# A graph-quantile layer whose engine order is planned: new durations, an order of readers of a PSUM tile, two more pairs scaled on VectorE, and the first sign tiles on ScalarE

## The chip, the cores and the metric

The kernel runs on one core of a Trainium2 chip. The metric is the device time of one execution in microseconds (us); lower is better. The core has these engines: PE (TensorE, matmuls, with its weight load shown as PEld), DVE (VectorE), ACT (ScalarE), POOL (GpSimd), and SP (SyncE, which here only issues transfers). Every engine works through its own list of instructions in order, and waits on semaphores where an instruction needs what another engine makes.

## The reference: what is computed

The input is x (16 graphs, 1024 nodes, 64 values) and a symmetric adjacency with some 8 neighbours and the node itself per row. Cut to what matters:

```python
h = jnp.maximum(_layernorm(x, axis=-1), 0.0)
# drop edges of rows with many neighbours
rem = neigh & (sk > 1) & (rank % sk == sk - 1) & mask[:, :, None]
rem = rem | jnp.swapaxes(rem, 1, 2)
nd = where(rem, 0, adj) > 0
# per node and value: quantiles over the neighbours that are left
s = jnp.sort(where(nd[..., None], h[:, None], inf), axis=2)
for tau, w in zip((0.25, 0.5, 0.75), (0.25, 0.5, 0.25)):
    pos = tau * (nv - 1)
    agg += w * interpolate(s, pos)
# a small MLP and the residual
y = relu((h + agg) @ W1 + b1) @ W2 + b2
out = x + y * mask
```

## The kernel before

The 16 graphs are worked on one after another as batches, and two batches form a pair m (0 to 7). For each batch, `prepare` (L1733) strings these together:

- `load` (L898): eight adjacency tiles of 128 rows arrive by DMA (tile `at`, or `spare` for early ones). Each is turned into signs `sg`, by ACT (L910) or, for every other tile of batch 0 (`fast and t % 2`), by POOL (L908). PE transposes the signs into a PSUM tile `tp` (L917, L923), and ACT (L930), or DVE (L928) for half of the first batch, writes it as `ne`.
- `number` and `drop`: PE counts (`cp`, `nb`) and ranks the neighbours (`rk`, L987 and L992), ACT takes a distance `dist` (L997), DVE decides which edges go (`rem`, L998).
- `keep`: PE combines this with its transpose (`kp`, L1015), ACT writes `kept` (L1020), PE counts again (`code`, L1023), ACT packs the result (`pack`, L1028). `order` makes a permutation `perm` (DVE, L1069) that puts nodes with many neighbours first.
- `collect` (L1073): for each of eight groups k of 128 nodes, nine matmuls (L1090, L1094) fill a PSUM tile `codeP`, of which there are two buffers. ACT copies three parts of it out (`st` L1099, `own` L1103 and L1104), and DVE finds the largest keys (MAX8 L1109, MATCH_REPLACE L1111). From the keys DVE makes `found`, `cand` and at last `idx` (L1138), the list of neighbours.

`fetch` and `issue` then gather the neighbours' rows into tiles `g` (POOL's indirect DMAs, L1281, 952 of them). The groups k are cut into classes (0), (1,2,3), (4,5), (6,7) with ever fewer slots for neighbours; the first two classes are half 0 of the pair, the last two half 1. `aggregate` (L1445) does half 1 first and then half 0. In it `sort` (L1366) runs a network of compare and exchange over the slots on DVE (L1386, L1389, L1394), multiplies the sorted slots by coefficients, and lets PE add them up in a PSUM tile `acc` (L1415). The multiplication has two forms: one DVE TENSOR_TENSOR for several slots (L1411), or, with `by_act`, one ACT ACTIVATE for each 64 columns (L1409). `by_act` is `m >= ACTP`, and `ACTP` is 3, so pairs 0 to 2 multiply on DVE and pairs 3 to 7 on ACT. `opened` adds a one-column MEMSET of `pause` (L805) behind each such DVE operation. As soon as half 1 of a pair has been done, its tiles are gathered anew for the next pair. `aggregate_group` does the same once for eight graphs' longest lists (tile `gg`), and `mlp` (L1551) and `output` (L1602) end a batch.

`weave` interleaves, in the program, the aggregation of pair m−1 with the preparation of pair m+1. This program order isn't what the engines run. `arrange` (L644) reads every instruction emitted, makes a `Step` of each (L605) with a duration `busy` and a delay `lag` to its readers (`cost`, L617), and works out what each must wait for: `before` (must have finished) and `behind` (must have been placed). Then it walks through time once. At each moment, on each engine, the step that is ready and comes first in program order goes next. A ready list may be left for `PATIENCE` ns in favour of a much earlier step, and `PATIENCE` is 0.0. The sequence found is then fixed on every engine by order-only dependencies. So the durations written in `cost`, and the dependencies, decide in which order each engine runs. Two reads of a tile have no order among them in `before`.

Of the kernel before, what the change touches and what calls it, by code (L numbers as in the profile page):

```python
# [33 lines left out]
BF16 = mybir.dt.bfloat16  # L34
# [11 lines left out]
C = 64  # L46
# [24 lines left out]
GROUP = 8  # L71
SLICE = P // GROUP
SECOND = 14
PATIENCE, AHEAD = 0.0, 200


TURNED = (0, 1, 3, 2, 0, 1, 3, 2)
# [472 lines left out]


LOADB, KEEPB, NORMB = 0, 3, 3
ACTP, ACTB = 3, 13
ENGINES = ("PE", "ACT", "DVE", "POOL", "SP")
NAMES = {"PE": "PE", "DVE": "DVE", "Activation": "ACT", "Pool": "POOL", "SP": "SP"}

# [48 lines left out]
class Step:  # L605

    def __init__(self, ins, place):
        self.ins, self.place, self.kind = ins, place, type(ins).__name__
        self.engine = NAMES[str(ins.engine).split(".")[-1]]
        self.reads, self.writes = (  # L610
            [Use(a.bass_ap) for a in aps if getattr(a, "bass_ap", None) is not None] for aps in (ins.ins, ins.outs)
        )
        self.moves = self.kind == "InstDMACopy"
        self.before, self.behind, self.after, self.tail = set(), set(), [], []
        self.busy, self.lag = self.cost()

    def cost(self):  # L617
        sides = self.writes + self.reads
        most = max([u.count for u in sides] or [1])
        if self.engine == "PE":  # L620
            n, lines = self.writes[0].count, self.writes[0].lines
            if any(u.size == 4 for u in self.reads):
                busy = 60 + n if n < 512 else 850
            else:
                busy = max(25, n / 2.4 + 3)
            return busy * 1.15 / (4 if lines[1] - lines[0] <= 32 else 2 if lines[1] - lines[0] <= 64 else 1), 200
        if self.engine == "ACT":
            columns = sum(u.count == 1 and u.size == 4 for u in self.reads) if most > 1 else 0
            return 55 + 0.87 * most + 75 * columns + (170 if len(self.writes) > 1 else 0), 150
        if self.engine == "DVE":  # L630
            psum = any(u.psum for u in sides)
            wide = [u for u in self.reads if u.count > 1]
            if self.kind == "InstTensorTensor" and all(u.size == 2 for u in sides):
                most /= 2
            elif self.kind in ("InstTensorScalarPtr", "InstTensorCopy") and not psum and len(wide) < 2:
                most = most / (4 if max(u.size for u in wide + self.writes) == 2 else 2) + 60
            return (most + 66) / 0.96 + (60 if psum else 0), 80
        if self.engine == "POOL":
            return (1330, 950) if self.moves else (300 if most <= 128 else 1000, 100)
        by = self.writes[0].size * self.writes[0].count * (self.writes[0].lines[1] - self.writes[0].lines[0])  # L640
        return 480, 1500 + by / 300


def arrange(tc, runs, loose, tails, paced):  # L644
# [15 lines left out]
    for s in steps:  # L660
        for u in s.reads + s.writes:
            name = u.tile.name
            for o, other in written.get(name, ()):
                if u.meets(other):
                    s.before.add(o.place)
            if u in s.writes:
                for o, other in read.get(name, ()):
                    if u.meets(other):
                        s.before.add(o.place)
        for u in s.writes:  # L670
            for table in (written, read):
                table[u.tile.name] = [e for e in table.get(u.tile.name, ()) if not u.covers(e[1])]
            written[u.tile.name].append((s, u))
        for u in s.reads:
            read.setdefault(u.tile.name, []).append((s, u))
        for u in s.reads + s.writes:
            if getattr(u.tile, "tag", None):
                if u.tile.name not in users:
                    order.setdefault(u.tile.tag, []).append(u.tile)
                users.setdefault(u.tile.name, []).append(s)  # L680
# [16 lines left out]
    for s in steps:  # L697
        s.behind -= s.before
        s.before.discard(s.place)
        s.behind.discard(s.place)  # L700
        s.left, s.ready = len(s.before) + len(s.behind), 0.0
        for p in (*s.before, *s.behind):
            steps[p].after.append(s)

    free, wire = dict.fromkeys(ENGINES, 0.0), 0.0
    waiting, able, sequence = ({e: [] for e in ENGINES} for _ in range(3))
    for s in steps:
        if not s.left:
            heappush(waiting[s.engine], (0.0, s.place))
    done = 0  # L710
    while done < len(steps):
        when, e = min(
            (free[e] if able[e] else max(free[e], waiting[e][0][0]), e) for e in ENGINES if able[e] or waiting[e]
        )
        while waiting[e] and waiting[e][0][0] <= when:
            heappush(able[e], heappop(waiting[e])[1])
        s = steps[heappop(able[e])]
        if waiting[e] and waiting[e][0][0] < when + PATIENCE and waiting[e][0][1] < s.place - AHEAD:
            heappush(able[e], s.place)
            free[e] = waiting[e][0][0]  # L720
            continue
        done += 1
        sequence[e].append(s)
        free[e] = when + s.busy
        if e == "SP":
            wire = max(wire, free[e]) + s.lag - 1500
            s.lag = wire + 1500 - free[e]
        for o in s.after:
            if s.place in o.behind:
                least = when  # L730
            else:
                least = free[e] + (s.lag + 60 if o.engine != e or s.moves else 115 if e == "DVE" else 0)
            o.ready = max(o.ready, least)
            o.left -= 1
            if not o.left:
                heappush(waiting[o.engine], (o.ready, o.place))
        for q in ENGINES:
            while waiting[q] and waiting[q][0][0] <= free[q]:
                heappush(able[q], heappop(waiting[q])[1])

    for k, s in enumerate(s for s in sequence["POOL"] if s.ins.name in paced[1]):
        if k > 1:
# [16 lines left out]
def list_layer(  # L759
# [138 lines left out]
    def load(b, fast=False):  # L898
# [4 lines left out]
        for t in range(NT):  # L903
            ask(b, t)
            at = asked.pop((b, t))
            sg = wk.tile([P, N], BF16, name="sg")
            if fast and t % 2:
                nc.gpsimd.tensor_scalar(sg, at, 0.0, None, OP.is_gt)  # L908
            else:
                nc.scalar.activation(sg, at, AF.Sign)  # L910
            ask(*divmod(b * NT + t + 2, NT))
            for n in range(2):
                tp = psum.tile([P, 4, P], F32, name="tp", tag="mx", bufs=3)
                run = []
                for s in range(4):
                    m = 4 * n + s
                    run.append(nc.tensor.matmul(  # L917
                        tp[:, s], sg[:, m * P:(m + 1) * P], ident16, start=(s == 0), stop=(s == 3 and t // 4 != n),
                        skip_group_check=True,
                    ))  # L920
                if t // 4 == n:
                    run.append(
                        nc.tensor.matmul(tp[:, t % 4], minus16, ident16, start=False, stop=True, skip_group_check=True)  # L923
                    )
                settle(run)
                to = ne[:, 4 * n:4 * n + 4, t * P:(t + 1) * P]
                if b <= LOADB and n:
                    nc.vector.tensor_scalar(to, tp, 0.0, None, OP.max, saturate=False)  # L928
                else:
                    nc.scalar.activation(to, tp, AF.Relu, saturate=False)  # L930
            if fast and t == 3:
                number(b, 0, 4)
            yield 0.1
# [139 lines left out]
    def collect(b, parts=((0, NT),)):  # L1073
# [12 lines left out]
        for first, last in parts:  # L1086
            for k in range(first, last):
# [5 lines left out]
                for t in range(NT):  # L1093
# [2 lines left out]
                        skip_group_check=True,  # L1096
                    ))
                settle(run)
                nc.scalar.copy(st[:, k], flat[:, OWN:VALUES])  # L1099
                halves, bytes_ = (  # L1100
                    own[:, k, b % 2].bitcast(d).rearrange("p (c k) -> p c k", c=C) for d in (BF16, U8)
                )
                nc.scalar.copy(halves[:, :, 1], flat[:, VALUES:VALUES + C])  # L1103
                nc.scalar.copy(bytes_[:, :, 0:2], flat[:, VALUES + C:].rearrange("p (c k) -> p c k", k=2))  # L1104
                left = code[:, :, :16]
                rest = wk.tile([P, NT, 16], F32, name="rest", bufs=1)
                lo, hi = PASSED[k], PASSED[k + 1]
                for at in range(lo, hi, 8):
                    nc.vector.max(keys[:, at:at + 8], left)  # L1109
                    if at + 8 < hi:  # L1110
                        nc.vector.match_replace(rest, keys[:, at:at + 8], left, 0.0)  # L1111
                        left = rest
                yield 0.4 * (hi - lo) / 4 - 0.4

            part = slice(PASSED[first], PASSED[last])
# [880 lines left out]
```

## Time and profile before

| | |
|---|---|
| Time, median of 9 runs | 2614.96 us (2608.6 to 2624.9) |
| The profiled execution: its time | 2607.81 us |
| The profiled execution: its span | 2605.9 us |
| Instructions | 30392 |
| Mean granted TensorE clock | 0.709 |
| DMA | 121.68 MB, 47 GB/s on average |
| ACT multiplications (L1409) | 560, 148.0 us, mean 350 ns |
| DVE multiplications of `g` (L1411) | 69, of 256 or 384 columns |
| DVE exchanges (L1389, L1394) | 659 each, 309.7 and 308.3 us |
| Sign tiles: on ACT, on POOL | 124, 1063 ns median; 4, 2766 to 2785 ns |

The span is what the profiler saw from the first to the last instruction; the time is of the same execution, with what lies around it. In a profile a row of a group reads: line, engine, operation, out<-in with shapes, x count | busy us, mean ns of one | idle us of the engine just before, and what ended most of it. "remote" in such a place is a semaphore update that comes from nothing the profile shows. The chain of waits follows the work that ended last back through time.

### The profile page before, as it was taken

The numbers are of one execution on the slowest core, as the hardware profiler recorded it, in microseconds if no ns is written. First come the engines' busy times: TensorE is split into PE (matmuls) and PEld (weight loads), VectorE is DVE, ScalarE is ACT, GpSimd is POOL, SyncE is SP. The second block draws the span as 40 slices with busy tenths as digits, with TensorE's granted clock in tenths as the row PEclk, the third lists the DMA queues.
The fourth block names the chain that finished last, engine by engine and source line by source line (L and its number), as shares of the span: only waits on it lengthen the run. The fifth ranks groups of instructions, "written<-read, shape, count | busy, mean of one in ns | idle before, by whom it ended". The sixth has DMA issues, their size and how long they took to land.

```text
span 2605.9 us, 30392 instructions
## 1 busy us (share of the span) xinstructions
PE 1226.3 (47%) x9011; PEld 762.2 (29%) x9011; DVE 1204.5 (46%) x5777; ACT 1109.5 (43%) x3089; POOL 966.3 (37%) x995
## 2 busy tenths in 40 slices
PE   7154346154806283163825436165392352653456
PEld 4133123032404141142413213153151121342334
DVE  5123167143507372193507704078373170529496
ACT  6154255144606262253606625056382242513375
POOL 1714432553262417415370244602507424430400
PEclk9577678586958586585958658576695675876778
DMA  5222122121212121122212112121121001100000
GB/s 171 63 76 68 39 72 60 37 57 49 59 29 86 19 64 40 41 74 52 60 27 80 44 18 60 25 67 37 46 61 42 16 14 22 31 16 1 17 17 11
DMA packets 128833, 121.68 MB, mean 47 GB/s; under 512 B 95730, under 2 KB 96274, under 8 KB 128658
## 3 DMA queue, kind: packets, MB, share of 16 engines
q1 hardware_dynamic: 97106, 87.29, 11.2%
q0 software_dynamic: 31552, 32.36, 6.3%
q8 instruction: 73, 1.20, 0.2%
q14 instruction: 102, 0.84, 0.1%
HBM read 108.79 MB, written 9.05 MB: 45 GB/s over the span
## 4 chain that ended last, share of the span: by engine, by line
another core or an unknown queue 28%; ACT 17%; PE 17%; issue 16%; DVE 6%; DMA 0%; DVEq 0%; SPq 0%; ACTq 0%
ACT dist L997 3%; PE codeP L1094 3%; ACT g L1409 2%; PE acc L1415 2%; ACT kept L1020 2%; ACT sg L910 2%; DVE g L1394 2%; ACT ne L930 1%; DVE g L1389 1%; PE rk L992 1%; PE tp L917 1%; PE rk L987 1%; PE kp L1015 1%; PE high L1537 1%
## 5 line engine op out<-in xcount | busy, mean ns | idle before, releaser
L1281 POOL DMA_INDIRECT g<-gtab,idx x952 | 920.6, 967 | 1393.7 <-issue 725.2
L1389 DVE TENSOR_TENSOR g<-g 128x256 f32<-128x256 f32 (+3 forms) x659 | 309.7, 491 | 63.6 <-PE tp L917 30.7
L1394 DVE TENSOR_TENSOR g<-g 128x256 f32<-128x256 f32 (+3 forms) x659 | 308.3, 490 | 22.4 <-remote 8.5
L997 ACT ACTIVATE dist<-rk,bias 128x512 f16<-128x512 f32 x256 | 169.9, 698 | 271.9 <-remote 198.0
L930 ACT ACTIVATE ne<-tp 128x512 fp8e4<-128x512 f32 x248 | 141.1, 607 | 318.2 <-remote 245.4
L917 PE MATMUL tp<-kb,sg 128*128 128x128 bf16 x1024 | 118.0, 257 | 292.1 <-ACT dist L997 143.3
L987 PE MATMUL rk<-kb,cnt 128*128 128x512 bf16 x256 | 120.0, 469 | 276.7 <-ACT dist L997 138.3
L998 DVE TENSOR_SCALAR rem<-dist,half 128x1024 bf16<-128x1024 f16 x128 | 62.6, 490 | 377.5 <-ACT dist L997 368.9
L1094 PE MATMUL codeP<-pack,perm 128*128 128x332 bf16 x1024 | 198.7, 339 | 11.8 <-DVE perm L1069 11.7
L1020 ACT ACTIVATE kept<-kp 128x512 fp8e4<-128x512 f32 x224 | 135.0, 616 | 144.8 <-remote 88.4
L992 PEld LDWEIGHTS <-ne 128*128 128x128 fp8e4 x1024 | 96.3, 115 | 341.4 <-issue 322.6
L917 PEld LDWEIGHTS <-sg 128*128 128x128 bf16 x1024 | 89.1, 118 | 318.5 <-issue 188.1
L1409 ACT ACTIVATE g<-g,coef 128x64 f32<-128x64 f32 x560 | 148.0, 350 | 56.7 <-DVE g L1389 38.2
L1415 PE MATMUL acc<-g,kf 128*128 128x128 f32 (+2 forms) x472 | 137.9, 425 | 54.2 <-ACT g L1409 37.3
L1023 PE MATMUL code<-kw,kept 128*128 128x17 fp8e5 x1024 | 65.2, 173 | 137.8 <-ACT kept L1020 74.7
L910 ACT ACTIVATE sg<-at 128x1024 bf16<-128x1024 f32 x121 | 126.6, 1075 | 3.6 <-DMA at<-in_adj_dram 3.5
L992 PE MATMUL rk<-kw,ne 128*128 128x128 fp8e5 x1024 | 126.1, 254 | 0.0
L1109 DVE MAX8 keys<-codeP 128x8 f32<-128x128 f32 x128 | 37.9, 296 | 189.0 <-ACT own L1104 92.8
L1094 PEld LDWEIGHTS <-perm 128*128 128x128 bf16 x1024 | 99.3, 107 | 81.5 <-DVE perm L1069 30.4
L805 DVE MEMSET pause<- 128x1 bf16 x1997 | 117.8, 59 | 3.0 <-issue 3.0
L1099 ACT CAST st<-codeP 128x4 bf16<-128x4 f32 x128 | 21.4, 167 | 225.6 <-remote 111.4
L1023 PEld LDWEIGHTS <-kept 128*128 128x128 fp8e4 x1024 | 52.1, 97 | 195.5 <-ACT kept L1020 112.6
(204 smaller groups left out, 2612.4 us busy)
## 6 DMA issues: line engine op xcount, KB each, us to landing
at<-in_adj_dram SPq DMA_DIRECT2D x122, 512.0 KB
g<-gtab,idx POOLq DMA_INDIRECT x952
xt<-in_x_dram SPq DMA_DIRECT2D x16, 256.0 KB
y<-in_x_dram SPq DMA_DIRECT2D x16, 256.0 KB
gtab<-xt SPq DMA_DIRECT2D x16, 256.0 KB
out_dram<-y SPq DMA_DIRECT2D x14, 256.0 KB
spare<-in_adj_dram SPq DMA_DIRECT2D x6, 512.0 KB
gg<-g SPq DMA_DIRECT2D x32, 48.0 KB
```

The costliest lines, as they stand in the source:

```text
L910: nc.scalar.activation(sg, at, AF.Sign)
L917: run.append(nc.tensor.matmul(tp[:, s], sg[:, m * P:(m + 1) * P], ident16, start=(s == 0), stop=(s == 3 and t // 4 != n), skip_group_check ...
L930: nc.scalar.activation(to, tp, AF.Relu, saturate=False)
L992: run.append(nc.tensor.matmul(rk[:, s * P:(s + 1) * P], ne[:, 4 * n + s, ts], upper, start=False, stop=(s == 3), skip_group_check=True,))
L997: nc.scalar.activation(dist[:, n * HALF:(n + 1) * HALF], rk, AF.Abs, bias=bias[:, t:t + 1])
L1020: nc.scalar.activation(kept[:, 4 * n:4 * n + 4], kp, AF.Relu, saturate=False)
L1094: run.append(nc.tensor.matmul(flat, perm[:, t, k * P:(k + 1) * P], pack[:, t], start=False, stop=(t == NT - 1), skip_group_check=True,))
L1281: ins = nc.gpsimd.indirect_dma_start(out=gathered[m, tiles][:, slot, k - lo, h], out_offset=None, in_=tables[2 * m + h][0], in_offset=bass ...
L1389: nc.vector.tensor_tensor(at(f + k * df, df, many), pa, pb, OP.min if what == "<" else OP.max)
L1394: nc.vector.tensor_tensor(pa if back else pb, pa, pb, OP.max if what == "<" else OP.min)
L1409: nc.scalar.activation(v[:, i, j], v[:, i, j], AF.Copy, scale=w[:, i, j:j + 1])
L1415: nc.tensor.matmul(acc, ident32, lines[:, s], start=False, stop=(s == now[-1] and not ends), skip_group_check=True)
```

## The change

It has four parts.

1. `ACTP` becomes 5: pairs 3 and 4 also multiply on DVE.
2. The four sign tiles of batch 0 that POOL made are made by ACT.
3. In `collect`, DVE's MAX8 and MATCH_REPLACE on a `codeP` tile are emitted ahead of ACT's three copies.
4. In `arrange`, reads of one PSUM tile are put in program order: an earlier read by another engine must have finished, one by the same engine must have been placed. With part 3, ACT's copies of a `codeP` tile so come after DVE's reads of it. The durations in `cost` are changed for float32 matmuls, ACT, and POOL. The walk is written anew as `spread`, used by `forward` and `backward`; with `ROUNDS` at 1 it runs forward once with ranks equal to program order, and what `backward` returns isn't used. `PATIENCE` and `AHEAD` go.

```diff
-PATIENCE, AHEAD = 0.0, 200
+ROUNDS = 1
...
-ACTP, ACTB = 3, 13
+ACTP, ACTB = 5, 13
...
         self.busy, self.lag = self.cost()
+        self.load = self.lag - 1500
...
-                busy = 60 + n if n < 512 else 850
+                busy = 4 * max(56, n / 2.4)
...
-            return 55 + 0.87 * most + 75 * columns + (170 if len(self.writes) > 1 else 0), 150
+            inside = 0 if any(u.psum for u in self.reads) else 45
+            return 50 + 0.83 * most + 93 * columns + inside + (170 if len(self.writes) > 1 else 0), 150
...
-            return (1330, 950) if self.moves else (300 if most <= 128 else 1000, 100)
+            return (1345, 950) if self.moves else (300 if most <= 128 else 4100, 100)
...
+def spread(steps, waits, ranks, place):
+
+    free = dict.fromkeys(ENGINES, 0.0)
+    waiting, able = ({e: [] for e in ENGINES} for _ in range(2))
+
+    def free_to_go(p, ready):
+        heappush(waiting[steps[p].engine], (ready, ranks[p], p))
+
+    for s in steps:
+        if not waits[s.place]:
+            free_to_go(s.place, 0.0)
+    for _ in steps:
+        when, e = min(
+            (free[e] if able[e] else max(free[e], waiting[e][0][0]), e) for e in ENGINES if able[e] or waiting[e]
+        )
+        while waiting[e] and waiting[e][0][0] <= when:
+            heappush(able[e], heappop(waiting[e])[1:])
+        s = steps[heappop(able[e])[1]]
+        free[e] = when + s.busy
+        place(s, when, free_to_go)
+    return max(free.values())
...
-            if u in s.writes:
-                for o, other in read.get(name, ()):
-                    if u.meets(other):
-                        s.before.add(o.place)
+            for o, other in read.get(name, ()) if u in s.writes or u.psum else ():
+                if u.meets(other):
+                    (s.before if u in s.writes or o.engine != s.engine else s.behind).add(o.place)
...
-    free, wire = dict.fromkeys(ENGINES, 0.0), 0.0
...
+    ranks, best = [float(s.place) for s in steps], None
+    for _ in range(ROUNDS):
+        sequence, starts, total = forward(steps, ranks)
+        if best is None or total < best[0]:
+            best = total, sequence
+        ranks = backward(steps, starts)
+    sequence = best[1]
...
-            if fast and t % 2:
-                nc.gpsimd.tensor_scalar(sg, at, 0.0, None, OP.is_gt)
-            else:
-                nc.scalar.activation(sg, at, AF.Sign)
+            nc.scalar.activation(sg, at, AF.Sign)
...
-                nc.scalar.copy(st[:, k], flat[:, OWN:VALUES])
-                halves, bytes_ = (
-                    own[:, k, b % 2].bitcast(d).rearrange("p (c k) -> p c k", c=C) for d in (BF16, U8)
-                )
-                nc.scalar.copy(halves[:, :, 1], flat[:, VALUES:VALUES + C])
-                nc.scalar.copy(bytes_[:, :, 0:2], flat[:, VALUES + C:].rearrange("p (c k) -> p c k", k=2))
                 left = code[:, :, :16]
...
                         left = rest
+                nc.scalar.copy(st[:, k], flat[:, OWN:VALUES])
+                halves, bytes_ = (
+                    own[:, k, b % 2].bitcast(d).rearrange("p (c k) -> p c k", c=C) for d in (BF16, U8)
+                )
+                nc.scalar.copy(halves[:, :, 1], flat[:, VALUES:VALUES + C])
+                nc.scalar.copy(bytes_[:, :, 0:2], flat[:, VALUES + C:].rearrange("p (c k) -> p c k", k=2))
```

More of the change, by code (lines that the diff above doesn't have):

```diff
@@ new lines, in between, with forward, place @@
+def between(s, o):
+    return s.lag + 60 if o.engine != s.engine or s.moves else 115 if s.engine == "DVE" else 0
+def forward(steps, ranks):
+    left, ready = [len(s.before) + len(s.behind) for s in steps], [0.0] * len(steps)
+    starts, sequence, wire = [0.0] * len(steps), {e: [] for e in ENGINES}, [0.0]
+    def place(s, when, free_to_go):
+        starts[s.place] = when
+        sequence[s.engine].append(s)
+        end = when + s.busy
+        if s.engine == "SP":
+            wire[0] = max(wire[0], end) + s.load
+            s.lag = wire[0] + 1500 - end
+        for o in s.after:
+            ready[o.place] = max(ready[o.place], when if s.place in o.behind else end + between(s, o))
+            left[o.place] -= 1
+            if not left[o.place]:
+                free_to_go(o.place, ready[o.place])
+    total = spread(steps, list(left), ranks, place)
+    return sequence, starts, total
@@ new lines, in backward, with place @@
+def backward(steps, starts):
+    left, ready, ends = [len(s.after) for s in steps], [0.0] * len(steps), [0.0] * len(steps)
+    def place(s, when, free_to_go):
+        ends[s.place] = when + s.busy
+        for p in (*s.before, *s.behind):
+            o = steps[p]
+            ready[p] = max(ready[p], when + s.busy - o.busy if p in s.behind else when + s.busy + between(o, s))
+            left[p] -= 1
+            if not left[p]:
+                free_to_go(p, ready[p])
+    spread(steps, list(left), [-(starts[s.place] + s.busy) for s in steps], place)
+    return [-t for t in ends]
@@ L700, in arrange @@
         s.behind.discard(s.place)
-        s.left, s.ready = len(s.before) + len(s.behind), 0.0
         for p in (*s.before, *s.behind):
             steps[p].after.append(s)
-    free, wire = dict.fromkeys(ENGINES, 0.0), 0.0
[L706 to L713, printed above, removed]
-        )
[L715 to L730, printed above, removed]
-            else:
[L732 to L739, printed above, removed]
+    ranks, best = [float(s.place) for s in steps], None
[5 more added lines that the diff above has]
+    sequence = best[1]
     for k, s in enumerate(s for s in sequence["POOL"] if s.ins.name in paced[1]):
@@ L906, in load @@
             sg = wk.tile([P, N], BF16, name="sg")
-            if fast and t % 2:
-                nc.gpsimd.tensor_scalar(sg, at, 0.0, None, OP.is_gt)
-            else:
-                nc.scalar.activation(sg, at, AF.Sign)
+            nc.scalar.activation(sg, at, AF.Sign)
             ask(*divmod(b * NT + t + 2, NT))
@@ L1098, in collect @@
                 settle(run)
-                nc.scalar.copy(st[:, k], flat[:, OWN:VALUES])
-                halves, bytes_ = (
-                    own[:, k, b % 2].bitcast(d).rearrange("p (c k) -> p c k", c=C) for d in (BF16, U8)
-                )
-                nc.scalar.copy(halves[:, :, 1], flat[:, VALUES:VALUES + C])
-                nc.scalar.copy(bytes_[:, :, 0:2], flat[:, VALUES + C:].rearrange("p (c k) -> p c k", k=2))
                 left = code[:, :, :16]
```

## The prediction

> **What bounds it.** I read the page's busy shares first, then the groups, then cut the span at the ends of the gathers and asked for the busy time of each stretch.
>
> ```profile
> PE 1226.3 (47%) x9011; PEld 762.2 (29%) x9011; DVE 1204.5 (46%) x5777; ACT 1109.5 (43%) x3089; POOL 966.3 (37%) x995
> ...
> another core or an unknown queue 28%; ACT 17%; PE 17%; issue 16%; DVE 6%; DMA 0%; DVEq 0%; SPq 0%; ACTq 0%
> ...
> L1281 POOL DMA_INDIRECT g<-gtab,idx x952 | 920.6, 967 | 1393.7 <-issue 725.2
> ...
> L1409 ACT ACTIVATE g<-g,coef 128x64 f32<-128x64 f32 x560 | 148.0, 350 | 56.7 <-DVE g L1389 38.2
> ...
> L1109 DVE MAX8 keys<-codeP 128x8 f32<-128x128 f32 x128 | 37.9, 296 | 189.0 <-ACT own L1104 92.8
> ```
>
> No engine is half busy, and over a quarter of the chain belongs to no visible queue. The 952 gathers come in 22 bursts, one gather per 1.25 to 1.33 us, about 1264 us in all. In a burst the rest nearly stands still, as waits such as this show:
>
> ```profile
> 752.26 0.43 DVE L1611 TENSOR_TENSOR yp<-yp,mask 128x256 f32<-128x256 f32 x1 [41.31 <-remote]
> ```
>
> The matmul it reads ended at about 711, and DVE moved only after the burst of 693 to 777 was well under way. Sorting, which waits for no matmul, does run in bursts. So the time is 1264 us of gathers, which the change leaves alone, and about 1342 us between them. That part is to be read. Columns: stretch, length, then busy us (count) of PE, PEld, DVE, ACT, POOL, then clock, DMA share, GB/s.
>
> ```profile
> 1084.20:1158.70 74.50, 45.31 (x415) 31.34 (x414) 59.71 (x310) 42.94 (x91) 0.00 (x0) 0.80 0.26 77
> 1221.80:1254.10 32.30, 26.99 (x267) 16.96 (x267) 20.81 (x110) 27.04 (x76) 0.00 (x0) 0.87 0.21 68
> ...
> 1373.60:1480.00 106.40, 59.42 (x496) 38.41 (x496) 93.23 (x463) 78.22 (x233) 0.00 (x0) 0.76 0.20 61
> 1540.50:1569.90 29.40, 23.06 (x222) 14.24 (x223) 3.14 (x19) 23.31 (x74) 0.00 (x0) 0.82 0.07 20
> ...
> 1688.70:1806.50 117.80, 78.29 (x523) 54.19 (x523) 90.45 (x564) 58.78 (x156) 0.00 (x0) 0.69 0.17 51
> 1870.20:1953.10 82.90, 71.46 (x534) 41.63 (x533) 58.37 (x290) 70.62 (x226) 0.00 (x0) 0.93 0.19 53
> ```
>
> Rows 1 and 2 are pair 2, which scales on DVE already; 3 and 4 are pair 3, 5 and 6 pair 4, which scale on ACT. The long stretches end when half 1 of the previous pair is sorted, scaled and accumulated, since its tiles are then refetched. DVE is 88% busy in row 3 and 77% in row 5; in rows 4 and 6 ACT and PE lead.
>
> **Part 1: pairs 3 and 4 scale on DVE.** ACT loses 224 of 560 activations. In a row they start 0.238 us apart (16 in 3.92 us), so 53 us. DVE gets 46 multiplies, 26 of 256 columns and 20 of 384; such rows already stand at 414 and 549 ns and repeat every 0.345 and 0.48 us, so 26×0.345 + 20×0.48 = 18.6, with the 46 pauses about 20 us. By the Trainium skill ("ScalarE: Activation LUTs", Rules for kernel authors) a multiply belongs on VectorE; by the rule alone the sum is 20−53 = −33 us. The rows say that it depends on the stage, so I price the four.
>
> Row 3 (end of half 1, 1471 to 1480):
>
> ```profile
> 1471.08 0.41 DVE L1394 TENSOR_TENSOR g<-g 128x256 f32<-128x256 f32 x1
> ...
> 1470.80 3.92 ACT L1409 ACTIVATE g<-g,coef 128x64 f32<-128x64 f32 x16
> ```
>
> ACT finishes 3.2 us after DVE's last exchange. On DVE the last multiplies follow at once. The planned order puts half 1's last DVE work at the same sum of DVE durations from the start (644 us before and after), because half 0's sorting is moved back behind it: −3.
> Row 4: 35 scales, 35×0.238 = 8.3 us of ACT's 23.3, go to a DVE with 3 us of work; PE at 23.1 then leads, so of 8.3 at most 29.4−24 = 5: −4.
> Row 5, chain of waits:
>
> ```profile
> 1782.43 5.47 ACT g L1409 x23
> ...
> 1797.02 3.93 ACT g L1409 x16
> ```
>
> 9.4 us of ACT scaling on the path become 12 multiplies, 12×0.345 = 4.1: −5.3. Against it DVE has 12 us more to do up to there (775 to 787), of which some slides into the burst before: I take −4, ends −8 and +6.
> Row 6: 64 scales at 0.238 = 15.2 us leave an ACT that is 85% busy; PE is at 71.5 of 82.9, so at most 11: −6.
> Sum of the part: −17.
>
> Against it speaks the Trainium skill ("SBUF — State Buffer", Who interferes with whom): a DVE instruction with two SBUF inputs contends with a GpSimd instruction that reads SBUF, and the gathers read their indices. If each of 46 multiplies held a gather for its length, that is 26×0.414+20×0.549 = 21.7 us. The rows of two bursts of 48 gathers:
>
> ```profile
> 1480.00:1540.50 60.50, 9.65 (x71) 4.86 (x69) 1.99 (x8) 10.11 (x17) 45.32 (x48) 0.55 0.19 43
> ...
> 1806.50:1870.20 63.70, 12.45 (x86) 8.37 (x86) 27.50 (x124) 22.79 (x64) 48.49 (x48) 0.58 0.21 51
> ```
>
> 25.5 us more DVE work go with 3.2 us more burst, 0.125 per us. 20 us cost then at most 2.5; half of it in bursts: +1. The row decides, being the same two instructions.
>
> **Part 2: first sign tiles.**
>
> ```profile
> 18.61 1.05 ACT L910 ACTIVATE sg<-spare 128x1024 bf16<-128x1024 f32 x1
> ...
> 18.75 2.77 POOL L908 TENSOR_SCALAR sg<-spare 128x1024 bf16<-128x1024 f32 x1 [1.33 <-DMA at<-in_adj_dram]
> ...
> 21.57 0.80 PE L917 MATMUL tp<-kb,sg 128*128 128x128 bf16 x8 [1.18 <-POOL sg L908]
> ```
>
> The last POOL tile delays PE until 21.57. On ACT it follows the 18.61 one and ends near 20.7: −1 (0 to −2). The first three are hidden by the adjacency DMAs that land between. ACT's queue takes 4×1.06 us more, with the ne evictions behind it (idle there by 0.5 to 1.3 us a tile); POOL's next work is the first gather at 67 us.
>
> **Part 3: readers of codeP.** DVE's keys take 296 ns from PE directly instead of after ACT's three copies (DVE idled 92.8 us, 60 times, behind L1104). ACT's st then waits behind DVE: queued behind it are ACT's other copies, ne, kept and scales, for which PE waits. Per tile DVE gains about 0.5 us; the release of the PSUM buffer is the same sum. The search is bound by PE and two buffers, so only the last tile of a batch pays: 0.5 us at some 14 batches whose idx gate a burst, minus what ACT waits: −5, ends −8 and +12 (8 tiles of a batch times 0.3 us for 5 batches in DVE-bound stages).
>
> **Part 4: the planner.** PATIENCE was 0, so its branch never acted; ROUNDS is 1 with ranks equal to program order, so the new walk is the old one with other durations and the added reader edges. The order of gathers is the old one but for a few of pair 1; SP exchanges x, output and table loads only locally, and DMA is not on the chain (0%). On DVE half 1 of pairs 5 and 6 ends 13 and 16 us of work later although about 20 were added before it: 4 to 7 us relatively earlier, half in the path: −4. The remaining shuffling I cannot price: 0 ± 15.
>
> Sum: −17 + 1 − 1 − 5 − 4 = −26. From the profiled execution's 2607.81 us (span 2605.9, so 1.9 around it) this gives 2582. The median of nine shown, 2614.96, is 7 above it: a run of the ordinary kind could stand at 2589; I stay with 2582 and let the range take it in. 0.2%, some 5 us, is what a measurement can tell from nothing.
>
> **Rivals.**
> 1. *Larger gain.* Pairs 3 and 4 shrink to pair 2's lengths. Pair 2: 74.5+32.3+20.8 = 127.6. Pair 3: 106.4+29.4+20.8 = 156.6. Pair 4: 200.7 less some 45 of one-time group aggregation = 155.7. 29+28 less gives 2551. For: pair 2 is the same work scaled on DVE. Against: rows 3 and 5 are long from DVE's own sorting. 0.15.
> 2. *DVE becomes the bound: slower.* Its place is row 3 and row 5. If the multiplies of both halves stand ahead of half 1's last exchange, 10 us enter each, less the 3 and 5 of ACT's tail: +12. ACT, in order, waits at codeP for a saturated DVE (the +12 of part 3, less the 4 won elsewhere): together +15 to +20, 2625. For: 93.2 of 106.4. Against: the planned order keeps half 1 in place. It decides when row 3's DVE passes 100 of its length. 0.29.
> 3. *Nothing.* Gathers and PE set the stages, ACT's share was cover: within 5 us, 2608. For: PE at 71.5 of 82.9. Against: 9.4 us of scaling on the chain. 0.11.
>
> My forecast has 0.45, its own range 2568 to 2598. Low 2550 takes rival 1's centre, high 2623 most of rival 2; two in ten stay out. Faster: 0.45 less 0.02, plus 0.15, plus 0.02 of rival 3: 0.60; same 0.09; slower 0.31.
>
> **What would show it.** Right: L1409 at x336, L1411 with 46 more; row 3's stretch 3 us shorter with DVE no busier, row 6's near 75 with PE leading; no ACT scaling on the chain before 1806; keys waiting for PE, st for DVE; gathers still 1264 us. Wrong: row 3 or 5 longer with DVE above 95%; ACT idle on "DVE keys" or "rest" by tens of us; bursts split or moved; more than 10 us of change in stages of pairs 0 to 2 or 6 and 7, which would be the order's doing alone.

## The result and the profile after

The changed kernel took 2552.88 us (median of 10 runs, 2540.96 to 2560.27); the kernel before, measured beside it, 2616.32 us (31 runs). The ratio is 0.9753, with a 95% interval from 0.9734 to 0.9772. The profiled execution took 2548.48 us, 59.3 less than the profiled one before.

The page of the changed kernel; its lines, with L1445 further down, answer to the five shown of the kernel before:

```profile
PE 1220.8 (48%) x9011; PEld 763.1 (30%) x9011; DVE 1221.9 (48%) x5869; ACT 1059.2 (42%) x2869; POOL 960.3 (38%) x991
...
another core or an unknown queue 34%; PE 19%; ACT 19%; issue 17%; DVE 10%; DMA 1%; DVEq 0%; SPq 0%; ACTq 0%
...
L1317 POOL DMA_INDIRECT g<-gtab,idx x952 | 916.8, 963 | 1357.6 <-issue 764.6
...
L1139 DVE MAX8 keys<-codeP 128x8 f32<-128x128 f32 x128 | 36.9, 294 | 174.1 <-issue 78.6
```

The multiplications by shape, DVE's in the kernel before, then DVE's and ACT's in the changed one:

```profile
L1411 DVE TENSOR_TENSOR g<-g,coef 128x384 f32<-128x384 f32 x30 | 15.4, 549 | 0.0
L1411 DVE TENSOR_TENSOR g<-g,coef 128x256 f32<-128x256 f32 x39 | 14.7, 414 | 0.0
```

```profile
L1447 DVE TENSOR_TENSOR g<-g,coef 128x384 f32<-128x384 f32 x50 | 26.3, 552 | 3.1 <-issue 3.0
L1447 DVE TENSOR_TENSOR g<-g,coef 128x256 f32<-128x256 f32 x65 | 24.6, 418 | 0.0
L1445 ACT ACTIVATE g<-g,coef 128x64 f32<-128x64 f32 x336 | 86.8, 341 | 34.3 <-DVE g L1425 17.0 <-DVE g L1430 10.6 <-DVE pause L844 4.8
```

The counts are the forecast ones (560 − 224 = 336, 69 + 46 = 115), and so are the durations. ACT is 50 us less busy, DVE 17 more, and the gathers cost the same. MAX8 no longer waits for ACT's copies, but DVE's idle time before it fell only from 189.0 to 174.1 us. And ACT's `st` now waits for DVE, as the list of waits of the changed kernel shows (total us, times, longest):

```profile
ACT st L1143 <- DVE rest L1141: 97.5, 40, 15.4
ACT st L1143 <- DVE keys L1139: 39.4, 32, 10.3
DVE keys L1139 <- PE codeP L1130: 48.9, 46, 14.2
```

Yet none of these rows says where 59 us went. The stretches between the bursts do. The windows view of the changed kernel, columns as before, for the stretches that answer to rows 3 to 6 of the prediction, and for two of pairs 5 and 6:

```profile
1354.00:1458.00 104.00, 60.56 (x495) 40.20 (x495) 91.76 (x460) 59.29 (x154) 0.03 (x1) 0.77 0.18 57
1519.50:1545.30 25.80, 19.50 (x211) 11.27 (x211) 4.62 (x25) 18.55 (x45) 0.04 (x1) 0.82 0.19 53
1664.90:1777.70 112.80, 70.38 (x503) 50.53 (x503) 91.83 (x573) 44.76 (x94) 0.00 (x0) 0.69 0.17 51
1840.10:1924.80 84.70, 73.72 (x581) 44.91 (x581) 72.10 (x354) 64.76 (x179) 0.00 (x0) 0.94 0.21 61
2029.70:2087.00 57.30, 34.15 (x207) 20.10 (x208) 41.09 (x221) 30.37 (x119) 0.00 (x0) 0.69 0.01 2
2268.70:2368.70 100.00, 63.96 (x433) 50.37 (x433) 90.02 (x433) 42.83 (x155) 0.00 (x0) 0.76 0.02 3
```

The two last stretches of the kernel before, not shown until now:

```profile
2055.70:2128.40 72.70, 47.46 (x291) 25.90 (x292) 48.36 (x257) 41.41 (x154) 0.04 (x1) 0.74 0.01 1
...
2310.20:2422.80 112.60, 61.93 (x435) 49.33 (x436) 93.95 (x445) 45.36 (x167) 0.02 (x1) 0.73 0.01 3
```

Since both kernels gather in the same sequence but for a few of pair 1, the start of the n-th gather is a clock for comparing them. From such points in both traces the sum is:

| Part of the span | before, ends at | after, ends at | gain in this part |
|---|---|---|---|
| to the second burst (batches 0 to 2) | 220.7 | 204.6 | 16.1 |
| to the long stretch of pair 3 (pairs 0 to 2) | 1373.6 | 1354.0 | 3.5 |
| pair 3 | 1688.7 | 1664.9 | 4.2 |
| pair 4 | 1953.1 | 1924.8 | 4.5 |
| pair 5 and what follows | 2310.2 | 2268.7 | 13.2 |
| long stretch of pair 6 | 2422.8 | 2368.7 | 12.6 |
| the end | 2605.9 | 2546.8 | 5.0 |

Pairs 3 and 4, the only ones whose multiplication moved, gave 8.7 of the 59.1 us. 41.9 came from the start and from pairs 5 and 6, where only the order of the work differs, and, at the start, four sign tiles.

One thing has to be known to read the experiments. They ran in three groups, on chips that the record numbers 0, 8 and 14, and there the same kernel before took 1516.16, 1514.81 and 1513.92 us, with the other engines at work while the gathers run. The record gives no number for the chip of the result above. Below, "the first chip" is where the result was measured, and "the second chip" is any of these three. Each experiment is compared by its ratio with the kernel before of its own group. It carries over to the first chip only where the traces from there show the same. The forecasts of the first experiments name times of the first chip, so these results can be held against them only roughly.

### The profile page after: what moved, and what is told of

Its sections match the earlier page's. It is cut to its first block, busy times and chain, and to the rows that moved or that the text cites. A ratio compares the mean times of both kernels' runs of the same rounds, so it can differ in the third digit from the quotient of the medians.

```text
span 2546.8 us, 30177 instructions
## 1 busy us (share of the span) xinstructions
PE 1220.8 (48%) x9011; PEld 763.1 (30%) x9011; DVE 1221.9 (48%) x5869; ACT 1059.2 (42%) x2869; POOL 960.3 (38%) x991
## 4 chain that ended last, share of the span: by engine, by line
another core or an unknown queue 34%; PE 19%; ACT 19%; issue 17%; DVE 10%; DMA 1%; DVEq 0%; SPq 0%; ACTq 0%
PE codeP L1130 4%; ACT dist L1033 4%; ACT sg L946 3%; DVE g L1425 2%; ACT ne L966 2%; DVE g L1430 2%; PE acc L1451 2%; ACT kept L1056 2%; PE kp L1051 1%; PE kp L1047 1%; ACT g L1445 1%; PE kp L1046 1%; PE tp L953 1%; PE rk L1028 1%
## 5 line engine op out<-in xcount | busy, mean ns | idle before, releaser
L1430 DVE TENSOR_TENSOR g<-g 128x384 f32<-128x384 f32 (+2 forms) x659 | 308.8, 490 | 29.1 <-remote 15.3
L1425 DVE TENSOR_TENSOR g<-g 128x256 f32<-128x256 f32 (+2 forms) x659 | 310.3, 491 | 22.7 <-remote 10.4
L1451 PE MATMUL acc<-g,kf 128*128 128x128 f32 (+2 forms) x472 | 144.4, 439 | 74.4 <-DVE pause L844 28.5
L1139 DVE MAX8 keys<-codeP 128x8 f32<-128x128 f32 x128 | 36.9, 294 | 174.1 <-issue 78.6
L1451 PEld LDWEIGHTS acc<-g,kf 128*128 128x128 f32 x472 | 85.0, 218 | 100.9 <-issue 32.3
L1647 DVE TENSOR_TENSOR yp<-yp,mask 128x256 f32<-128x256 f32 x32 | 13.7, 428 | 200.7 <-remote 136.1
L1046 PE MATMUL kp<-ne,kw 128*128 128x512 fp8e4 x256 | 100.9, 394 | 12.1 <-ACT dist L1033 10.9
```

The costliest lines, as they stand in the source:

```text
L1046: nc.tensor.matmul(kp, plus, ne[:, 4 * n:4 * n + 4, ts], start=True, stop=False),
L1425: nc.vector.tensor_tensor(at(f + k * df, df, many), pa, pb, OP.min if what == "<" else OP.max)
L1430: nc.vector.tensor_tensor(pa if back else pb, pa, pb, OP.max if what == "<" else OP.min)
L1451: nc.tensor.matmul(acc, ident32, lines[:, s], start=False, stop=(s == now[-1] and not ends), skip_group_check=True)
```

## The experiments

All edits but the rewritten walk, put into the kernel before, give exactly the changed kernel's instructions in the same order on all five engines. So the rewritten walk itself adds nothing. Part 3 without the reader edges wasn't tried, nor the edges without part 3.

**Part 1 alone.**

```diff
-ACTP, ACTB = 3, 13
+ACTP, ACTB = 5, 13
```

> The kernel before with ACTP = 5 alone: no other durations, no reader order, sign tiles and codeP readers as before. Theory A (the gain lies in the multiplications that leave ACT): most of the 63 us, below 2580, and the stretches before the bursts of pairs 3 and 4 shorter by some 25 us each. Theory B (the order found with new durations and reader edges carries it): -5 to -15 us, in pairs 3 and 4 alone. Theory C (DVE becomes the bound): not faster.

Measured: 1517.37 against 1516.16 us, ratio 1.0018 (1.0001 to 1.0035). Theory A falls on this chip; B expected a gain and there is none. C's "not faster" came true, but the run doesn't show that DVE took over as the bound, as the rival meant it.

**All but part 1.**

```diff
-ACTP, ACTB = 5, 13
+ACTP, ACTB = 3, 13
```

> The changed kernel with ACTP back at 3: part 1 alone undone. Theory A: near 2610. Theory B: 2560 to 2570, the start and pairs 5 and 6 as short as in the changed kernel and only the stretches of pairs 3 and 4 longer.

Measured: 1461.28 us, 0.964 (0.9621 to 0.966). The whole change gives 0.9647 (below), so part 1 adds nothing in this company either. A falls a second time; so does B's small loss without part 1.

**Part 2 alone.**

```diff
-            if fast and t % 2:
-                nc.gpsimd.tensor_scalar(sg, at, 0.0, None, OP.is_gt)
-            else:
-                nc.scalar.activation(sg, at, AF.Sign)
+            nc.scalar.activation(sg, at, AF.Sign)
```

> The kernel before with the four sign tiles of batch 0 on ACT, nothing else. Theory D (the 16 us won before the second burst are the sign tiles'): the first gather near 61 and the second burst's first near 205, -10 to -16 us in all. Theory B: -1 us, first gather near 66.

Measured: 1508.39 us, 0.9953 (0.9938 to 0.9967): 7.8 us. The first gather moved from 68.9 us (in the kernel with part 1 alone) to 62.8. So the 6 us at the first gather are the sign tiles', as D said. Its −10 to −16 in all is missed in microseconds, though as a ratio to the first chip's time it holds. The 16 us before the second burst are not shown to be theirs, and B's −1 was too little.

Why 6 and not 1? The timeline of ACT in this kernel:

```profile
15.86 1.07 ACT L907 ACTIVATE sg<-spare 128x1024 bf16<-128x1024 f32 x1
...
17.29 1.07 ACT L907 ACTIVATE sg<-spare 128x1024 bf16<-128x1024 f32 x1
```

The timeline of PE in the kernel with part 1 alone, whose start is that of the kernel before:

```profile
22.35 1.04 PE L917 MATMUL tp<-kb,sg 128*128 128x128 bf16 x8 [0.97 <-POOL sg L908]
```

and of PE in the kernel with part 2 alone:

```profile
18.41 0.62 PE L914 MATMUL tp<-kb,sg 128*128 128x128 bf16 x8 [0.75 <-ACT sg L907]
```

Tiles that stand on POOL for 2.77 us delay PE more than once. The last two sign tiles of the `spare` buffers start on ACT at 15.86 and 17.29; in the kernel with part 1 alone one started at 19.60 on ACT and the other at 19.50 on POOL. That POOL's earlier tiles pushed the later ones back is read from these times. The last transposes come 3.9 us earlier; the other 2 us of the 6 weren't traced.

**Part 3 with the reader edges of part 4.**

```diff
-            if u in s.writes:
-                for o, other in read.get(name, ()):
-                    if u.meets(other):
-                        s.before.add(o.place)
+            for o, other in read.get(name, ()) if u in s.writes or u.psum else ():
+                if u.meets(other):
+                    (s.before if u in s.writes or o.engine != s.engine else s.behind).add(o.place)
...
-                nc.scalar.copy(st[:, k], flat[:, OWN:VALUES])
...
                         left = rest
+                nc.scalar.copy(st[:, k], flat[:, OWN:VALUES])
...
```

> The kernel before with parts 3 and the reader edges of part 4 (DVE reads codeP first, and the plan knows that readers of a PSUM tile follow one another), the old durations, ACTP 3, POOL's sign tiles. Theory B1 (readers' order and the plan's knowledge of it carry the order's gain): -25 to -50 us, with pairs 5 and 6 shortened by 15 and 12. Theory B2 (the new durations carry it): within 10 us of before.

Measured: 1489.39 us, 0.9838 (0.9815 to 0.986), −27 us. That is in B1's range of microseconds, at its small end, and outside B2's 10 us. The cost moved as forecast: ACT's `st` now waits for DVE. This is the list of waits of that kernel:

```profile
ACT st L1106 <- DVE rest L1104: 72.2, 36, 10.9
```

**The whole change, on the second chip.**

> The changed kernel itself, beside the kernel before on the same chip as the other runs. On the chip of the last runs the kernel before took 1516 us, its gathers ran through nearly without a break and other engines worked beside them; there the changed kernel with ACTP at 3 took 0.964 of it. Theory B (the order carries it, ACTP next to nothing): 0.955 to 0.970 there, ratio 0.975 where the gathers come in bursts. Theory A (ACT's multiplications): below 0.945.

Measured: 1460.62 against 1514.81 us, 0.9647 (0.9624 to 0.9671): B's range. The windows of the end show where it lies. First the kernel with part 1 alone, then the changed one, each from POOL's 952nd indirect transfer to the end. That count includes transfers for other tiles than `g`; 34 gathers still follow it in both:

```profile
1347.70:1518.60 170.90, 115.69 (x555) 72.61 (x555) 130.58 (x421) 104.45 (x277) 59.59 (x35) 0.76 0.08 17
```

```profile
1353.70:1453.60 99.90, 54.13 (x258) 32.92 (x257) 74.10 (x198) 57.68 (x167) 46.86 (x35) 0.76 0.11 24
```

The changed kernel reaches this point 6 us later, but 62 us of PE's work and 56 us of DVE's, which the other still has before it, are done by then. Its last gather then starts at 1403.9 instead of 1421.8 us, and the other 47 us of the gain come after it. The last instruction that makes `idx`, the list of neighbours, started at 1191.5 us instead of 1239.7. This lead grew over the batches, though not at each: 8 us at the first, 14 at the fourth, 27 at the tenth, 48 at the last.

**The durations alone.**

```diff
-                busy = 60 + n if n < 512 else 850
+                busy = 4 * max(56, n / 2.4)
...
-            return 55 + 0.87 * most + 75 * columns + (170 if len(self.writes) > 1 else 0), 150
+            inside = 0 if any(u.psum for u in self.reads) else 45
+            return 50 + 0.83 * most + 93 * columns + inside + (170 if len(self.writes) > 1 else 0), 150
...
-            return (1330, 950) if self.moves else (300 if most <= 128 else 1000, 100)
+            return (1345, 950) if self.moves else (300 if most <= 128 else 4100, 100)
```

> The kernel before with the new durations alone (PE float32, ACT, POOL). Theory B2 (durations carry the order's gain): 0.975 to 0.985, and together with the 0.984 of readers and edges they make up the 0.964 of all parts without ACTP. Theory B1 (knowing the order of readers carries it): 0.995 to 1.005.

Measured: 1474.62 us, 0.9733 (0.9712 to 0.9754). B1's range for this run is missed; B2 holds and its range was a little too careful. The parts don't add up as B2 had it: 0.9838 × 0.9733 × 0.9953 × 1.0018 = 0.955, where the whole measured 0.9647.

**All but the durations** (the same diff turned round, in the changed kernel).

> The changed kernel with the old durations in the plan. Theory B2: 0.02 to 0.025 above the changed kernel's ratio. Theory B1: within 0.006 of it.

Measured: 1486.96 us, 0.982 (0.9797 to 0.9842), 0.017 above the changed kernel: nearer to B2, a little below its range, and outside B1's. So on the second chip the durations carry 2.7% alone and 0.017 of the ratio on top of the rest, and part 3 with the reader edges 1.6% alone.

**Which duration?** Each alone, in the kernel before: that of PE's float32 matmuls, that of ACT, that of POOL.

> The kernel before with one new duration: float32 matmuls, 4*max(56, n/2.4) for 60+n. All three together gave 0.9733 where the gathers run without a break. A matmul of 128 columns goes from 216 to 258 ns in the plan, one of 64 from 143 to 258 (both with the factor 1.15); measured are 439 ns as a row and 0.14 to 0.27 us apart. If the place of the accumulations carries the gain: 0.980 or below. If not: 0.995 to 1.005.

> The kernel before with one new duration: ACT. A scale of 64 columns in SBUF goes from 186 to 241 ns in the plan, where the chip starts one per 238 ns; an eviction of 512 columns from 500 to 475 ns, where the chip starts one per 480. If ACT's true price of the 560 scales is what the old plan lacked, this carries the gain: 0.975 to 0.985. If the gain is luck of one order among many: anything from 0.97 to 1.01, not near the sum of parts.

> The kernel before with one new duration: POOL, 1345 for 1330 ns a gather and 4100 for 1000 ns a large operation. Gathers are 1.1% dearer in the plan, so it changes order little: 0.995 to 1.005 by either theory.

Measured: PE 0.9935 (0.9918 to 0.9952), ACT 0.9828 (0.981 to 0.9847), POOL 1.0098 (1.0079 to 1.0117). PE's lies between its two forecasts (the 439 ns in them is the mean of rows of three widths). ACT's is as forecast for a true price, but it lies in the range for luck too. POOL's misses its range on the slow side: a gather dearer by 1.1% in the plan, with large POOL operations at 4100 ns, costs 14 us. The 4100 ns are no truer than the 1000 before: the sign tiles took 2766 to 2785 ns on POOL. The product is 0.986, the three together are 0.9733; that the parts don't add up is what luck had forecast. So a change of the plan that seemed to mean little moved this kernel by 1%. Of the three only ACT's effect is above that. That truer durations make a better order fits ACT's run, but isn't shown.

**Twelve rounds of the plan.**

```diff
-ROUNDS = 1
+ROUNDS = 12
```

> The changed kernel with ROUNDS = 12: the walk runs forward and back twelve times with ranks from the way back, and the shortest by its own durations is taken. If the plan's durations describe the chip, it beats the changed kernel by 0.01 or more; if the order's gain is luck of one order, it lies anywhere within 0.02 of it.

Measured: 1444.28 us, 0.954 (0.9521 to 0.956), 0.011 below the changed kernel with intervals apart: the fastest version here. Its window after POOL's 952nd indirect transfer:

```profile
1350.90:1439.20 88.30, 52.02 (x233) 32.72 (x233) 63.15 (x160) 39.29 (x132) 45.16 (x35) 0.73 0.11 21
```

Less work of DVE and ACT is left over than in the changed kernel, and as much of PE. Both forecasts allow this result, so it doesn't decide between them. No other number of rounds was run, and the 1% has the same caution on it as POOL's.

**Two chips, one kernel.** The kernel before without the wait between gathers:

```diff
-        if k > 1:
-            paced[1][s.ins.name].wait_op(paced[0], k - 1, "sem-ge")
+        pass
```

> The kernel before without the wait that lets a gather start only once the gather before it has been issued; order and work the same. It asks what parts the 2615 us of the profile shown before, with other engines standing in the bursts of gathers, from the 1515 us of these runs. If it is how many gathers are queued at once: far above 1515, towards 2600, with bursts and late matmul signals. If the chip differs in something else: 1480 to 1530, and gathers 1.25 to 1.35 us apart as before.

Measured: 1513.26 us, 0.9992 (0.9978 to 1.0006). Taking the wait away doesn't make the kernel slow on the second chip; on the first chip it wasn't tried. What parts 2615 from 1515 us is open.

## Why the prediction came out as it did

The time was in the range, near its lower end, and outside the likeliest case's own (2568 to 2598): −59 us where −26 was summed, on the profiled executions. That the time fell into the range is partly luck: the largest term, −17 for part 1, was to lie in four stretches that together gave 9.2, and the parts of the span outside pairs 3 and 4, where the sum had about −10, gave 50. Rival 1 named 2551, almost the time measured, by a mechanism that didn't happen: pairs 3 and 4 were to shrink by 57 us together and gave 8.7.

- *What bounds it.* Right for the first chip: the bursts take as long as before within some 6 us, and the gain lies between them. That other engines stand still in a burst was read as a property of the gathers. On the second chip PE, DVE and ACT work beside the same gathers (busy 75, 81 and 69% of the span with part 1 alone). It was a property of the first chip's runs.
- *Part 1, −17.* Too much. Rows 3 to 5 came within 1 us of their prices: −2.4, −3.6, −5.0 for −3, −4, −4. That part 1 did it there isn't shown, since the order changed too. Row 6 was to lose 6 us and grew by 1.8: ACT's 70.62 us fell only to 64.76, although 15 us of scaling had left it. The freed room was filled with other work; DVE's busy time there rose from 58.37 to 72.10. The step's "at most 11" took the stretch's contents as fixed, but the planner refilled them. In row 5 DVE's busy time hardly rose (91.83 for 90.45 us); in row 3 ACT lost 19 us and the stretch 2.4, so most of it had been cover. On the second chip part 1 is worth nothing by both experiments.
- *The two rules weighed.* A multiply was cheaper on VectorE, where the Trainium skill ("ScalarE: Activation LUTs", Rules for kernel authors) puts it: ACT's multiplications take 61.2 us less (86.8 for 148.0), DVE's 20.8 more (50.9 for 30.1). On the second chip that was worth nothing; being cheaper isn't being on the path. A cost of contention with the gathers' reads (the Trainium skill, "SBUF — State Buffer", Who interferes with whom) wasn't seen in the gathers: 963 ns each after, 967 before.
- *Part 2, −1.* Too little. The prediction let ACT's last tile start after the 18.61 one and called the first three hidden. In the changed kernel, on the first chip, the last `spare` tile's sign starts at 17.71, the first gather comes at 61.4 instead of 67.4, and part 2 alone gives 6 us at the first gather on the second chip. The other 10 us before the second burst lie in the first burst and the stretch behind it, here before and after:

```profile
67.40:146.80 79.40, 10.19 (x83) 5.84 (x82) 9.76 (x59) 12.26 (x31) 60.20 (x63) 0.54 0.22 51
146.80:220.70 73.90, 50.70 (x490) 34.91 (x490) 32.73 (x127) 50.14 (x111) 0.00 (x0) 0.85 0.28 87
```

```profile
61.40:148.80 87.40, 22.41 (x170) 14.41 (x169) 15.55 (x77) 25.87 (x60) 60.31 (x63) 0.60 0.29 76
148.80:204.60 55.80, 39.85 (x407) 27.16 (x407) 28.11 (x112) 36.24 (x90) 0.05 (x1) 0.90 0.26 77
```

The burst is 8 us longer, since it breaks off at 75.3 for 7.9 us, but 22.4 us of PE's work go with it instead of 10.2, and the stretch behind it is 18.1 us shorter. That the break is what let the work through fits the trace but wasn't tested.

- *Part 3, −5.* The idle time of 92.8 us behind ACT is gone, and `st` waits for DVE instead. Of DVE's idle time before MAX8 only 14.9 us went in all. Part 3's price can't be told from the reader edges'; the two together gave 27 us on the second chip.
- *Part 4, −4 and 0 ± 15.* This is the step that failed most. It called half 1 of pairs 5 and 6 a little earlier, half of it in the path, and the rest without a price. Their stretches lost 15.4 and 12.6 us. The burst and the stretch of pair 5, and all of the span up to the ends of both stretches, before and after:

```profile
1953.10:2055.70 102.60, 17.17 (x133) 9.24 (x133) 23.09 (x96) 15.36 (x25) 78.22 (x80) 0.55 0.17 38
0.00:2128.40 2128.40, 988.89 (x7558) 607.97 (x7559) 939.17 (x4692) 903.42 (x2518) 835.00 (x861) 0.70 0.20 53
0.00:2422.80 2422.80, 1125.96 (x8496) 701.53 (x8497) 1085.67 (x5410) 1013.89 (x2848) 932.72 (x962) 0.71 0.19 49
```

```profile
1924.80:2029.70 104.90, 19.97 (x179) 10.71 (x178) 23.46 (x105) 18.21 (x35) 77.91 (x80) 0.60 0.16 35
0.00:2087.00 2087.00, 972.08 (x7524) 603.33 (x7525) 953.09 (x4769) 846.23 (x2273) 820.76 (x856) 0.71 0.20 54
0.00:2368.70 2368.70, 1117.45 (x8496) 701.92 (x8497) 1102.19 (x5498) 960.92 (x2616) 917.82 (x957) 0.71 0.19 50
```

The stretch of pair 5 needs 84 fewer matmuls before its gate opens (291 to 207), 13.3 us less of PE. Of these 84, 46 ran in the burst ahead of it and 4 before that, and 34 were still to come: work was moved to both sides. For pair 6 none of PE's work was put off: 8496 matmuls start before the end of its stretch in both kernels. There DVE has 3.9 us less to do, and its idle time falls from 18.7 to 10.0 us. The walk being the old one was right and beside the point; on the second chip the durations alone gave 0.9733.

- *The signs it named.* Of the signs of being right, row 6 failed (84.7 us for "near 75"). Of the signs of being wrong, three came true. Bursts split, the first one by a break of 7.9 us. ACT idled 136.9 us for "DVE rest" and "keys", though in front of `st` it idled less in all, 171 us for 225. And the stages of pairs 0 to 2 changed by 19.6 us, the stretch of pair 6 by 12.6, which the prediction itself had called the order's doing alone.
- *The rivals.* Slower (0.29) fell: row 3's DVE is at 88% of its stretch, as before. "Nothing" was right about ACT's share and wrong about the whole, for it too looked at the multiplications only.

The second chip's runs show the order's share there, not on the first. That it is also the greater share on the first is read from where the gain lies in its traces; no part was run alone there.

## What to carry to other kernels

Where a planner orders the engines, price a change to its durations and edges as the main term, with a range of its own: here the duration of one engine moved the time by 1%, and all three by 2.7%. Work taken from a busy engine is worth only the wait that ends there last, and the planner may refill the room. To find a gain spread over a whole kernel, follow one sequence common to both traces, here the gathers and the lists they wait for.

## What was not expected of the hardware

The same kernel takes 2615 us where the result was measured and 1514 to 1516 us on the three chips of the experiments, with the same gathers and the same work. The median time from one gather to the next is 1.25 us in the slower trace and 1.26 in the other (part 1 alone), so a gather costs much the same. But the slower trace has 22 breaks of over 5 us between its gathers, and the other has 4. What differs are the waits for PE. Here is one entry of the list of waits, in the kernel before on the first chip, then with part 1 alone on the second:

```profile
DVE yp L1611 <- remote: 147.2, 7, 41.3
```

```profile
DVE yp L1611 <- PE yp L1607: 24.5, 19, 5.7
```

In the slower traces a wait for PE often ends only long after the matmul's end, and is then put down to "remote": ACT's `ne` waited 245.4 us so, and its `dist` 198.0. No trace of the second chip has a single wait for "remote". The cause is open. The mean granted clock is 0.709 on the first chip and 0.859 to 0.873 on the second for the same kernel; whether that is cause or effect wasn't tested. With the new durations alone the clock of the profiled execution is 0.899, and the same 9011 matmuls keep PE busy for 1124.7 us instead of 1146.5 (part 1 alone, clock 0.864).
